# Storing the last six row tiles of a two-layer graph kernel in pairs

## The chip, the cores and the metric

The kernel runs on one core of a Trainium2 chip. The metric is the device time of that core in microseconds, from launch to end, as a median over runs. The profile adds one profiled execution, in which every instruction and every DMA packet has a time; times in the text that look like 2147.05 count from the first instruction of that execution.

## The reference

Two layers work on 3327 nodes with 512 features and a 3327x3327 adjacency matrix `adj`. Each one normalises its input, takes the positive part and adds its result to the input. Cut to what matters:

```python
# layer 0: attention with the adjacency as a bias
h = jnp.maximum(_layernorm(x, axis=-1), 0.0)
q, k, v = h @ Wq.T + bq, h @ Wk.T + bk, h @ Wv.T + bv
a = q @ k.T * scale + adj + adj
x = x + softmax(a) @ v
# layer 1: normalised graph convolution
h = jnp.maximum(_layernorm(x, axis=-1), 0.0)
A2 = adj + eye(N); d = diagonal(A2) ** -0.5
temp = A2 @ h @ W.T
x = x + relu((d[:, None] * A2 * d[None, :]) @ temp)
```

All is float32. The change concerns only the last line, and of it only the last piece that is written to the output.

## The kernel before

The 3327 rows are padded to 26 row tiles of 128 rows, and the columns of every feature matrix are handled in 128-wide pieces. The adjacency is cut into two strips of 14 and 12 tiles, and each of the three large products with it is done by a seven-product scheme (the names p1 to p7): TensorE multiplies blocks, VectorE forms sums of blocks before and after. All of these are steps of one list, `steps`; the function `run(k)` emits step k together with loads, sums and stores that were attached to it.

The order on every engine is the order in which the Python code emits instructions: the whole list is emitted under `in_order`, which ties each instruction of VectorE, TensorE, GpSimd, ScalarE and SyncE to the one emitted before it on the same engine. So each engine, and each queue of DMA issues, works through a fixed sequence. DMAs are issued by SyncE (the page calls its queue q1) and ScalarE (q10).

Stores are emitted late. A store is put on the list `posted` with a step number, and `deliver(n)` emits those whose number is below n (line 799).

Most of the output is produced transposed and is turned back in blocks of 32 by VectorE: `Columns.turn`, `Columns.scale` and `Columns.add` (lines 1151, 1157 and 1160). `Columns.add` posts four stores to SyncE (line 1163), each of 32 partitions by 28 (or 24) runs of 32 numbers, that is 128 bytes a run. The last six row tiles, 20 to 25, columns 0 to 255, take another way, since nothing is left to hide theirs: when the last product is complete, VectorE adds its last banks (line 976), TensorE turns the six tiles into six PSUM banks (`turned`, line 1111), and `finish` does the rest for one tile: ScalarE takes the positive part with the row's scale (line 1124), VectorE adds the residual `xr` (line 1125), and a store is posted (line 1126). The loop that calls it deals the six stores out in turn:

```python
for n, i in enumerate(range(20, NT)):
    finish(i, nc.scalar if n % 2 else nc.sync)
deliver(len(steps) + 1)
```

So tiles 20, 22 and 24 are stored by SyncE and tiles 21, 23 and 25 by ScalarE. Each store moves 128 runs of 1 KB, one from each partition. The residuals were loaded in pairs well before (`last_load`), so nothing here waits for them.

The completion of DMAs issued by SyncE and ScalarE is counted on eight semaphores. The programming layer hands these out in turn, over both queues, in the order in which it schedules the issues; an issue whose semaphore was last given to an earlier transfer first waits until that transfer is complete. In the built program of before, the three ScalarE stores get three of the semaphores first. Four stores of the last `Columns.add` and one earlier one then take the next five, and the three SyncE stores come round to the same three as ScalarE's: the store of tile 20 waits for the completion of that of tile 21, tile 22 for tile 23, tile 24 for tile 25.

After the last store stands a conditional branch to a general version of the kernel for unusual inputs, which is not taken for these inputs: the engines jump over it. In the block that they jump to, SyncE waits for the eight semaphores one by one (line 1720), and then all engines meet twice (line 1715).

Of the kernel before, what the change touches and what calls it, by code (L numbers as in the profile page):

```python
# [11 lines left out]
AF = mybir.ActivationFunctionType  # L12
# [3 lines left out]
P = 128  # L16
# [31 lines left out]
def graph_layers_kernel(  # L48
# [30 lines left out]
    nc = tc.nc  # L79
    NP, D = x.shape  # L80
    DC = D // P
    NT = NP // P
    scale = 1.0 / math.sqrt(D)
    E = D // 2
# [16 lines left out]
    def ring(*slots):  # L101

        turn = itertools.cycle(slots)

        def take(shape, name):
            kind, k = next(turn)
            return kind(k, shape, name)

        return take

    @contextmanager
    def in_order(*engines):

        traced = nc.cur_bb.bb.instructions
        before = traced[-1]
        yield
        begin = next(k for k in reversed(range(len(traced))) if traced[k] is before) + 1
        last = {}
        for ins in traced[begin:]:
            if ins.engine in engines:  # L120
                if ins.engine in last:
                    tc.add_manual_dep(ins, last[ins.engine].name,
                                      mybir.DependencyInfo(mybir.DependencyClass.NoSync, mybir.DependencyReason.DATA),
                                      reason="in_order")
                last[ins.engine] = ins
# [96 lines left out]
    class Chain:  # L222
# [32 lines left out]
        @staticmethod  # L255
        def finish():
            if Chain.before:
                Chain.before()
            Chain.before = None
# [377 lines left out]
    with in_order(*(e.engine for e in (nc.vector, nc.tensor, nc.gpsimd, nc.sync))):  # L637
# [9 lines left out]
        k = len(steps)  # L647
# [64 lines left out]
    sd = const.tile([P, NT], F32, name="sd")  # L712
# [79 lines left out]
    now = [0]  # L792
    posted = []
# [4 lines left out]
    def deliver(before):  # L798
        while posted and posted[0][0] < before:
            posted.pop(0)[1]()  # L800
# [19 lines left out]
    out_last = ring((half, 12), (half, 13), *spare[2:], (half, 14))  # L820
# [277 lines left out]
    xrs = {}  # L1098
# [15 lines left out]
    turned_last = {}  # L1114
# [5 lines left out]

    def finish(i, queue):

        xr, pt, o = xrs[i], turned_last[i], out_last([P, D], "r")
        nc.scalar.activation(o[:, 0:E], pt[:, 0:E], AF.Relu, scale=sd[:, i : i + 1])
        nc.vector.tensor_add(o[:, 0:E], o[:, 0:E], xr)
        posted.append((now[0], lambda: queue.dma_start(out[i * P : (i + 1) * P, 0:E], o[:, 0:E])))

    class Columns:

# [41 lines left out]
    def number_of(g, r, s, t):  # L1171
        return ((g * len(ORDER) + r) * 2 + s) * len(every) + t
# [5 lines left out]
    for g in range(3):  # L1178
        for n, r in enumerate(ORDER):
            for t, e in enumerate(every):  # L1180
                k = number_of(g, n, 0, t)
# [9 lines left out]
    for n, job in enumerate(jobs):  # L1191
        k = k0 + n * (k1 - k0) // len(jobs)
# [10 lines left out]
    k = number_of(0, 5, 1, 2)  # L1203
# [6 lines left out]
    k = number_of(1, 5, 1, 2)  # L1210
# [8 lines left out]
    k = number_of(2, 4, 0, 0)  # L1219
# [12 lines left out]
    k = number_of(1, 4, 0, 0)  # L1232
# [105 lines left out]
    with in_order(*(e.engine for e in (nc.vector, nc.tensor, nc.gpsimd, nc.scalar, nc.sync))):  # L1338
        for k in range(len(steps)):
            run(k)  # L1340
        deliver(len(steps))
        now[0] = len(steps)
        for n, i in enumerate(range(20, NT)):
            finish(i, nc.scalar if n % 2 else nc.sync)
        deliver(len(steps) + 1)
    return flags[0]

# [376 lines left out]
```

## Time and profile before

| | us |
|---|---|
| median of three runs | 2160.23 (2158.45 to 2162.33) |
| the profiled execution's own time | 2159.13 |
| its span, first to last instruction | 2157.3 |
| TensorE busy | 2137.5 (99% of the span) |
| VectorE busy | 1652.0 (77%) |
| ScalarE busy | 273.1 (13%) |
| last TensorE instruction | starts at 2146.68 |
| last VectorE addition of line 1125 | starts at 2147.95 |

The profiled execution lies 1.8 us above its span, and 1.1 us below the median of the runs. TensorE is busy nearly throughout, and only in the last ten microseconds or so is it not. In the lists of instructions a "q" after an engine's name (SPq, ACTq) marks its sequencer, which issues DMAs and waits for semaphores; for a DMA the duration is that of the issue, and the landing is given apart.

### The profile page before, as it was taken

What the parts mean: (1) busy time and instruction counts of PE and PEld (TensorE: products, weight loads), DVE (VectorE), ACT (ScalarE), POOL (GpSimd) and SP (SyncE); (2) the same over time, 40 slices, a digit from 0 to 9 for tenths busy, and PEclk for the clock granted to TensorE, in tenths of its full rate; (3) what the DMA queues carried; (4) which work ended last, traced back from release to release, by engine and by line L of the source; (5) the groups of instructions that cost most, each with busy time, mean ns of one, the idle gap of its engine ahead of it and who ended that gap; (6) DMA issues with size and microseconds to landing.
All of it is one profiled execution on the core that took longest, in us unless ns stands there. A gap on an engine that the chain in (4) does not pass through costs nothing.

```text
span 2157.3 us, 20906 instructions
## 1 busy us (share of the span) xinstructions
PE 2137.5 (99%) x6272; PEld 1180.9 (55%) x6272; DVE 1652.0 (77%) x3235; ACT 273.1 (13%) x441; POOL 68.1 (3%) x63
## 2 busy tenths in 40 slices
PE   9999999999999999999999999999999999999998
PEld 5555555555555555555454555555666665555554
DVE  7479888888887688776777778886566576778897
ACT  6311211112110000001111000010111100000000
POOL 2000000000004000000111000000000000000000
PEclk9999999999999999999999999999999999999999
DMA  8678888888999899889787889986646578978996
GB/s 305 210 257 303 296 311 282 306 289 291 337 308 299 292 370 330 278 296 309 267 308 260 303 283 368 321 303 221 203 146 201 150 225 252 303 229 247 261 293 167
DMA packets 402546, 592.10 MB, mean 274 GB/s; under 512 B 140012, under 2 KB 273528, under 8 KB 402424
## 3 DMA queue, kind: packets, MB, share of 16 engines
q1 hardware_dynamic: 374488, 533.12, 75.2%
q10 hardware_dynamic: 27936, 57.56, 7.3%
q8 instruction: 52, 0.85, 0.2%
q14 instruction: 70, 0.57, 0.1%
HBM read 422.71 MB, written 173.87 MB: 277 GB/s over the span
## 4 chain that ended last, share of the span: by engine, by line
PE 93%; DVE 4%; DMA 2%; issue 1%; POOL 0%; ACT 0%; SPq 0%; DVEq 0%
PE p L919 55%; PE Y L542 13%; PE Z L542 6%; PE p L910 5%; PE p L1026 4%; PE pw L1087 3%; PE X L542 3%; PE Y L398 2%; PE Z L398 1%; DMA rows<-row 1%; DMA part<-sum 1%; PE X L398 0%; DMA wk<-in_wk_dram 0%; DVE part L164 0%; DVE st L185 0%
## 5 line engine op out<-in xcount | busy, mean ns | idle before, releaser
L919 PE MATMUL p<-part,b 128*128 128x448 f32 (+1 forms) x3528 | 1257.6, 513 | 0.8 <-DVE part L165 0.6
L919 PEld LDWEIGHTS p<-part,b 128*128 128x128 f32 x3528 | 669.9, 190 | 542.1 <-issue 291.8
L542 PE MATMUL Y<-qt,hp 128*128 128x448 f32 (+1 forms) x832 | 308.2, 513 | 2.6 <-DVE g L546 1.8
L164 DVE TENSOR_TENSOR part<-part 128x896 f32<-128x896 f32 (+1 forms) x252 | 256.5, 1018 | 68.8 <-DMA part<-sum 29.6
L542 PEld LDWEIGHTS Y<-qt,hp 128*128 128x128 f32 x832 | 157.8, 190 | 136.3 <-issue 72.7
L542 PE MATMUL Z<-qt,hp 128*128 128x384 f32 (+1 forms) x416 | 162.3, 512 | 0.0
L166 DVE TENSOR_TENSOR part<-part,part 128x448 f32<-128x448 f32 (+1 forms) x219 | 129.4, 591 | 15.3 <-DVE part L165 0.5
L165 DVE TENSOR_TENSOR part<-part,part 128x448 f32<-128x448 f32 (+1 forms) x219 | 129.4, 591 | 7.2
L910 PE MATMUL p<-part,b 128*128 128x448 f32 (+1 forms) x336 | 124.2, 512 | 0.0
L542 PEld LDWEIGHTS Z<-qt,hp 128*128 128x128 f32 x416 | 79.0, 190 | 66.2 <-issue 37.9
L546 DVE SCALAR_TENSOR_TENSOR g<-g,Y 128x384 f32<-128x384 f32 (+1 forms) x156 | 91.3, 585 | 29.9 <-PE Y L542 28.4
L962 ACT COPY part<-p 128x384 f32<-128x384 f32 (+1 forms) x33 | 16.6, 503 | 656.1 <-PE p L919 497.8
L910 PEld LDWEIGHTS p<-part,b 128*128 128x128 f32 x336 | 63.8, 190 | 54.1 <-issue 31.0
L549 ACT ACTIVATE g<-g 128x768 f32<-128x768 f32 (+1 forms) x48 | 43.0, 896 | 347.5 <-DVE g L546 311.7
L542 PE MATMUL X<-qt,hp 128*128 128x384 f32 (+1 forms) x208 | 81.1, 512 | 0.0
L963 DVE TENSOR_TENSOR part<-p,part 128x384 f32<-128x384 f32 (+1 forms) x33 | 19.3, 585 | 62.2 <-PE p L919 61.4
L1026 PE MATMUL p<-w,ct 128*128 128x512 f32 x136 | 61.6, 592 | 0.0
L542 PEld LDWEIGHTS X<-qt,hp 128*128 128x128 f32 x208 | 39.5, 190 | 33.1 <-issue 19.3
L191 POOL TENSOR_TENSOR rstd<-ve,mhalf 128x1 f32<-128x1 f32 x46 | 38.4, 836 | 529.5 <-DVE ve L189 502.2
L982 DVE TENSOR_TENSOR ct<-p,part 128x448 f32<-128x448 f32 (+1 forms) x72 | 42.3, 608 | 16.2 <-PE p L910 12.1
L1087 PE MATMUL pw<-w,rows 128*128 128x256 f32 x208 | 53.5, 380 | 0.4 <-DVE rows L1077 0.4
L1017 DVE TENSOR_TENSOR job<-job 128x896 f32<-128x896 f32 (+1 forms) x52 | 52.9, 1017 | 0.0
(194 smaller groups left out, 1679.0 us busy)
## 6 DMA issues: line engine op xcount, KB each, us to landing
part<-sum SPq DMA_DIRECT2D x104, 448.0 KB, 5.3
part<-p SPq DMA_DIRECT2D x91, 448.0 KB, 6.0
part<-sum SPq DMA_DIRECT2D x104, 384.0 KB, 4.1
part<-p SPq DMA_DIRECT2D x91, 384.0 KB, 4.6
part<-in_adjT_dram SPq DMA_DIRECT2D x78, 448.0 KB, 5.1
b<-row SPq DMA_DIRECT2D x234, 128.0 KB, 4.9
part<-in_adjT_dram SPq DMA_DIRECT2D x78, 384.0 KB, 3.9
g<-in_adjT_dram SPq DMA_DIRECT2D x52, 448.0 KB, 4.2
```

The lines of the kernel that those rows point to most:

```text
L164: yield nc.vector.tensor_add(o[:, 0:2], g[:, 0:4:3], g[:, 1:2].to_broadcast([P, 2, g.shape[-1]]))
L165: yield nc.vector.tensor_add(o[:, 2], o[:, 1], g[:, 0])
L166: yield nc.vector.tensor_add(o[:, 3], o[:, 2], g[:, 2])
L398: nc.tensor.matmul(ps[:, :w], M[B[name]][:, c, o * P : (o + 1) * P], hp[k][:, A[name], c], start=start and c == 0, stop=c == 1, skip_group ...
L542: nc.tensor.matmul(ps[:, :wd], h_of(self.t, name, k), qt[B[name]][:, k], start=start and k == 0, stop=k == 1, skip_group_check=True)
L546: nc.vector.scalar_tensor_tensor(a[n], a[n], 2.0, ps[:, :wd], op0=ALU.mult, op1=ALU.add if sign > 0 else ALU.subtract)
L549: nc.scalar.activation(g[1], g[1], AF.Exp, **({"bias": pad} if self.t == HALF - 1 else {}))
L910: yield nc.tensor.matmul(ps[("p2", "p3", "p4", "p8")[k]][:, :w], b[:, z], a[:, 0, y], start=k == 3 and not self.seeded, stop=True, skip_gr ...
L919: yield nc.tensor.matmul(ps[r][:, :w], b[:, i], m, start=self.t == 0 and not adds, stop=self.t == PAIRS - 1 and r in ("p1", "p5", "p6", "p ...
L1017: nc.vector.tensor_add(self.a, self.a, self.b)
L1026: nc.tensor.matmul(ps, cts[s][y][d][:, k * P : (k + 1) * P], w[d], start=d == 0, stop=d == DC - 1)
L1087: nc.tensor.matmul(ps, a, W[B[name]][:, c], start=new and c == 0, stop=c == 1, skip_group_check=True)
```

## The change

The six tiles are taken two at a time. `finish` now takes the first tile of a pair, computes both into one buffer of 128 x 2 x 256, and posts one store of both. The loop runs over tiles 20, 22 and 24: the pairs 20-21 and 22-23 are stored by SyncE, the pair 24-25 by ScalarE. The ScalarE and VectorE instructions keep their number, shapes and order.

```diff
     def finish(i, queue):
 
-        xr, pt, o = xrs[i], turned_last[i], out_last([P, D], "r")
-        nc.scalar.activation(o[:, 0:E], pt[:, 0:E], AF.Relu, scale=sd[:, i : i + 1])
-        nc.vector.tensor_add(o[:, 0:E], o[:, 0:E], xr)
-        posted.append((now[0], lambda: queue.dma_start(out[i * P : (i + 1) * P, 0:E], o[:, 0:E])))
+        o = out_last([P, 2, E], "r")
+        for k in range(2):
+            nc.scalar.activation(o[:, k], turned_last[i + k][:, 0:E], AF.Relu, scale=sd[:, i + k : i + k + 1])
+            nc.vector.tensor_add(o[:, k], o[:, k], xrs[i + k])
+        to = out[i * P : (i + 2) * P, 0:E].rearrange("(k p) e -> p k e", p=P)
+        posted.append((now[0], lambda: queue.dma_start(to, o)))
...
-        for n, i in enumerate(range(20, NT)):
-            finish(i, nc.scalar if n % 2 else nc.sync)
+        for i in range(20, NT, 2):
+            finish(i, nc.scalar if i == NT - 2 else nc.sync)
         deliver(len(steps) + 1)
```

In the built program this also changes which completion semaphore each of the last transfers has. Only three stores take one now. The pair 20-21 waits for a store of the last `Columns.add` but one that was issued at 2136.56 in the profiled execution, the pair 22-23 for the one issued at 2137.15, and the pair 24-25 for one older still. The first SyncE store of a pair waits for the second addition of line 1125, the other for the fourth, and ScalarE's for the sixth.

## The prediction

> **What bounds the kernel now.** I read the page's busy line first: TensorE is busy 99% of the span, and the chain of work puts 93% of it on TensorE. The change touches no TensorE instruction, so only the stretch after the last one can move, and I went to the timeline of that stretch, then to the waits of SyncE's queue, then to the three lines that end the kernel.
>
> From the page:
>
> ```profile
> span 2157.3 us, 20906 instructions
> PE 2137.5 (99%) x6272; PEld 1180.9 (55%) x6272; DVE 1652.0 (77%) x3235; ACT 273.1 (13%) x441; POOL 68.1 (3%) x63
> ```
>
> The timeline from 2136 to 2158 us (start, duration, engine, line, what):
>
> ```profile
> 2144.19 1.94 DVE L976 TENSOR_TENSOR part<-part,p 128x384 f32<-128x384 f32 x4
> ...
> 2146.13 2.25 DVE L1125 TENSOR_TENSOR r<-r,xr 128x256 f32<-128x256 f32 x6
> ...
> 2147.05 0.35 ACTq L1126 DMA_DIRECT2D out_dram<-r  x1
> 2147.06 0.86 ACT L1124 ACTIVATE r<-pt,sd 128x256 f32<-128x256 f32 x2
> 2147.68 1.44 ACTq L1126 DMA_DIRECT2D out_dram<-r  x2
> 2150.57 2.21 SPq L1126 DMA_DIRECT2D out_dram<-r  x3
> ```
>
> VectorE has added everything at 2148.38 (2146.13 + 2.25). SyncE's three stores are nevertheless issued only from 2150.57 on, though the first needs only the first addition, done at 2146.6. The waits of SyncE's queue from 2140 to 2158 us (in total, times, longest) say why:
>
> ```profile
> SPq L1126 <- DMA out_dram<-r: 3.8, 1, 3.8
> SPq L1720 <- SPq L1720: 2.6, 1, 2.6
> ```
>
> The first SyncE store waits 3.8 us for a DMA that stores an `r`. Line 1126, by itself:
>
> ```profile
> L1126 ACTq DMA_DIRECT2D out_dram<-r x3: 348/532/707, 2147.0 to 2148.4; - x3
> L1126 SPq DMA_DIRECT2D out_dram<-r x3: 351/377/1293, 2150.6 to 2151.5; - x3
> ...
> DMA to landing us min/median/max: 2.7/3.0/3.5
> ```
>
> ScalarE's first store is issued at 2147.05 and takes the longest, 3.5 us: it lands at 2150.55, and SyncE goes on at once. That is the shared completion semaphore: tile 20's store waits for tile 21's. Last, the lines of 1720:
>
> ```profile
> L1720 SPq EVENT_SEMAPHORE  x8: 17/17/17, 2155.4 to 2156.0; - x8
> ...
> L1720 SPq COMPARE_BRANCH  x1: 50/50/50, 2152.8 to 2152.8; - x1
> ```
>
> SyncE's last issue starts at 2151.49 and lasts 1.29, to 2152.78; the branch follows; 2.6 us later come the eight waits, and 1.3 us after the last of these (2156.0) the span ends at 2157.3. So the end is SyncE's last issue plus 4.5 us. The landing of that store, 2.9 us after its issue by the DMA view (2154.4), lies hidden behind the branch.
>
> **What the Trainium skill says.** "Runtime: NRT & Kernel Launch", Instruction fetch mechanics: a taken branch whose target isn't already fetched stalls for a fetch. The trace agrees: 2.6 us between branch and first wait on SyncE, and as much on ScalarE (2149.1 to 2151.7). "DMA: Bandwidth & Descriptors", Rules for kernel authors: issuing from several engines brings no bandwidth, since all run on the same 16 DMA engines. Here, 1 KB runs went at 250 per us from ScalarE's queue nearly alone (150 packets in 2149.4 to 2150.0) and at 267 from SyncE's alone (187 in 2151.4 to 2152.1); no stretch shows both with such runs at once. "Perfetto Trace Analysis", DMA Instruction — HWDGE: the time of an issue is descriptor generation and not the movement of data. Agreed: issues take 0.35 to 1.29 us, landings 2.7 to 3.5.
>
> **The change part by part.** ScalarE's six activations and VectorE's six additions stay as they are, so 2148.38 stays: nothing gained, nothing lost. The two-tile buffer costs no new wait, since the first activation waits for TensorE alone in both programs.
>
> *SyncE's wait of 3.8 us goes.* The pairs wait for column stores issued at 2136.56 and 2137.15; line 1163's landings take 7.7 us at most, so these are complete by 2145. What is late next is the addition. The pair 20-21 needs the second one, as ScalarE's first store does now, so it can start where that one starts, at 2147.05; SyncE's column stores are issued by then (the last starts at 2145.88 and takes 0.83: 2146.71). That costs the pair a later addition than tile 20 had, hidden as long as SyncE is busy until 2146.71, so 0.3 us at most. The pair 22-23 needs the fourth: 2147.68. ScalarE's pair needs the sixth: 2148.41.
>
> *Three SyncE issues become two, of twice the runs.* Stores of two runs from each partition are in the trace: line 534 takes 359/367/633 ns (least, median, most). With 0.37 each, SyncE is done at 2147.68 + 0.37 = 2148.05. Bounds: 0.36 from below, and from above 1.29, as before's last issue, which gives 2149.0. In before it was 2152.78: 4.7 us earlier. With the tail unchanged at 4.5 us the end would be 2152.6, and SyncE would reach its eight waits at 2148.05 + 2.65 = 2150.7.
>
> *The cover of the landings is now thin.* SyncE no longer gives the data 2.6 us more than they need. The DMA view counts 475 packets of SyncE's queue in 2148 to 2149 and 56 in the next: some 530 of the column stores' 128-byte runs are left at 2148.0. In 2147 to 2148, with the queue alone, 1248 went. So they are gone at 2148.4. Then come 6 x 128 = 768 runs of 1 KB. SyncE's queue has the engines alone until ScalarE's pair begins; a 1 KB store begins about 0.9 us after its issue (2150.57, none before 2151.3), so at 2149.3: 0.9 us x 267 = 240 runs. The other 528 share the engines. Alone, a queue kept them busy 69% (250 per us) and 75% (267), so two can reach 357 per us if they fill each other's gaps: 1.5 us, to 2150.8. If they don't, 528 / 260 = 2.0 us, to 2151.3. A landing is reported some 0.5 us after its last data (ScalarE's last: data thin out after 2150.5, landing 2148.41 + 2.7 = 2151.1). So all land between 2151.3 and 2151.8. The three semaphores concerned stand fourth to sixth of the eight; from the sixth to the end are 0.15 + 1.3 = 1.5 us. End between 2152.8 and 2153.3, and 2152.6 if landings don't show at all.
>
> *Sum.* The span of 2157.3 becomes 2152.6 to 2153.3, so 4.0 to 4.7 us less. I take 4.45, near the end where the two queues overlap, because each alone leaves a quarter of the engines' time unused. The profiled execution took 2159.13, so it would be 2154.7; the median is 1.1 above it: 2160.23 - 4.45 = 2155.8.
>
> **The rivals.**
>
> *A late landing takes the place of the wait.* Some of the 16 parts of a transfer come late. For it: line 1126's landings already spread over 0.8 us, and line 534's two-run stores take 4.7 us in the median and 8.1 at most; the three engines' branches fetch in these very microseconds. Against it: line 534 ran amid heavy traffic. With 4.7 us from 2147.68 or 2148.41 the landing is 2152.4 to 2153.1 and the end 2153.9 to 2154.6: 2.7 to 3.4 us gained, so 2157.2 us. With 8.1 from 2148.41 it is 2156.5, the end 2158.0, a loss of 0.7.
>
> *SyncE's issues stall behind the column stores: slower.* Issues of line 1163 took 2.57 at 2128.05 and 2.73 at 2130.66, when much was queued. At 2147.05 some 1780 runs are still queued. Two issues of 2.7 us end at 2152.45, still 0.3 us before 2152.78. It decides from 5.7 us for both on; with 5.49 each, the longest issue of any SyncE row (line 830), they end at 2158.0 and the kernel takes 2165.5. Against it: the fourth column store of the last group, issued at 2145.88 with most of the other three still queued, took only 0.83.
>
> *The wait stays.* If something else than the shared semaphore holds SyncE, the first pair goes at 2150.57, the second at 2150.94, done at 2151.3 instead of 2152.78: 1.5 us gained, 2158.7. Against it: the landing at 2150.55 fits too well.
>
> **How the numbers follow.** A measurement of this kernel can tell about 0.2%, 4.3 us, from no change; the first case lies across that bound. Its chance is 0.75, the late landing's 0.18, the stall's 0.04 and the wait that stays 0.03. In the first case the gain is 4.45 at best knowledge, a little over 4.3, and the medians scatter (the three runs by 3.9 us): I give 0.51 to over the bound and 0.24 to within it. With the late landing 0.03 is over it by scatter, 0.15 within. The stall counts as slower. So 0.54 faster, 0.42 same, 0.04 slower. The range: 4.0 to 4.7 widened by a scatter of 2 us gives 2153.5 to 2158.2, and the late landing and the wait that stays reach to 2158.7.
>
> **What would show it.** Right: no wait of SyncE's queue for an `r` store; its two issues near 2147.05 and 2147.7, its branch near 2148.1, and a wait at line 1720 of up to 1 us for landings. Late landing: that wait is longer. Stall: issues of over 1.3 us at line 1128. The forecast is wrong if the last TensorE instruction moves by more than a microsecond, or SyncE's first pair starts after 2149.

## The result, and the profile after

The changed kernel takes 2157.2 us in the median of 22 runs, against 2160.17 for 22 runs of the kernel before: a ratio of 0.9986, 95% interval 0.9981 to 0.9992. That is 3.0 us less, 1.7 to 4.1 by the interval: a gain, and one within the 0.2% (4.3 us) named in the prediction. Forecast were 2155.8 us in a range of 2153.5 to 2158.7.

The span of its profiled execution says much less:

```profile
span 2156.7 us, 20900 instructions
PE 2139.1 (99%) x6272; PEld 1180.4 (55%) x6272; DVE 1651.7 (77%) x3235; ACT 273.1 (13%) x441; POOL 68.0 (3%) x63
```

That is only 0.6 us under before's 2157.3, because the long stretch in front, which the change does not touch, differed from one execution to the other: the sixth addition of line 1126 ends at 2150.93 here, and ended at 2148.38 in before. What lies behind that addition is what the change can reach. I call the time from its end to the end of the span **the tail**, and give times of the tail as T+. The tail was 2157.34 - 2148.38 = 9.0 us before and is 2156.72 - 2150.93 = 5.8 us now: 3.2 us less, which fits the medians.

The timeline of the end of the changed kernel (start, duration, engine, line, what):

```profile
2148.68 2.25 DVE L1126 TENSOR_TENSOR r<-r,xr 128x256 f32<-128x256 f32 x6
2149.50 1.31 SPq L1128 DMA_DIRECT2D out_dram<-r  x2
2150.96 0.40 ACTq L1128 DMA_DIRECT2D out_dram<-r  x1
```

SyncE's two stores now begin while VectorE still adds, 1.4 us before the last addition ends; in before the first of three began at T+2.2. The waits of SyncE's queue from 2148 us on:

```profile
SPq L1722 <- SPq L1722: 3.9, 1, 3.9
SPq L1128 <- DVE r L1126: 1.0, 2, 0.5
```

The 3.8 us for another store's landing are gone. A store now waits for VectorE's additions, 0.5 us each time. But the branch, 2.6 us in before, stands at 3.9. Lines 1128 and 1722:

```profile
L1128 SPq DMA_DIRECT2D out_dram<-r x2: 554/568/583, 2149.5 to 2150.2; - x2
L1128 ACTq DMA_DIRECT2D out_dram<-r x1: 401/401/401, 2151.0 to 2151.0; - x1
...
DMA to landing us min/median/max: 3.9/3.9/3.9
```

```profile
L1722 SPq EVENT_SEMAPHORE  x8: 17/17/17, 2154.8 to 2155.3; - x8
...
L1722 SPq COMPARE_BRANCH  x1: 50/50/50, 2150.9 to 2150.9; - x1
```

SyncE branches at 2150.9 (T-0.1; in before T+4.5) and is at its eight waits at 2154.8 (T+3.9). It goes through them without a stop, one each 0.07 to 0.09 us. ScalarE's pair, issued at 2150.96, lands 3.9 us later, at 2154.85 (T+3.9). So the landings stay hidden, by some 0.3 us only, and the branch still sets the end.

### The profile page after: what moved, and what is told of

It is laid out like the page before. It is cut to its first block, busy times and chain, and to the rows that moved or that the text cites. A ratio compares the mean times of both kernels' runs of the same rounds, so it can differ in the third digit from the quotient of the medians.

```text
span 2156.7 us, 20900 instructions
## 1 busy us (share of the span) xinstructions
PE 2139.1 (99%) x6272; PEld 1180.4 (55%) x6272; DVE 1651.7 (77%) x3235; ACT 273.1 (13%) x441; POOL 68.0 (3%) x63
## 4 chain that ended last, share of the span: by engine, by line
PE 90%; DMA 5%; DVE 5%; issue 1%; POOL 0%; ACT 0%; SPq 0%; ACTq 0%; DVEq 0%
PE p L919 52%; PE Y L542 13%; PE Z L542 6%; PE p L910 5%; PE p L1026 4%; PE pw L1087 3%; PE X L542 3%; PE Y L398 2%; DMA rows<-row 1%; PE Z L398 1%; DMA part<-sum 1%; DMA t<-b 1%; DMA part<-p 1%; DVE part L164 1%; PE X L398 0%
```

## The experiments

Two theories on the gain: **the wait** on the shared completion semaphore was its cause, or **the number** of transfers (three instead of six) was. And two questions behind it: why the branch now takes 3.9 us, and what comes next if it goes.

**Does it repeat?** The changed kernel and the kernel before, once more each.

> The changed kernel once more, to see how far its one profile holds. I measure the tail: from the end of the sixth addition on VectorE to the end of the span, 8.9 us in the profile of before and 5.7 in that of the changed kernel. If the tail is settled by the program, it is 5.5 to 6.0 again, with 3.9 us between SyncE's branch and its first wait, and the median about 3 us under before. If the 3.9 us were a chance of one execution (2.6 in before), the tail is near 4.5 here.

Measured: ratio 0.9979 (0.9972 to 0.9986), 2155.41 against 2159.67 us, so 4.3 us less where the first measurement had 3.0. The tail is 6.1 us, and the branch is long again:

```profile
SPq L1722 <- SPq L1722: 4.3, 1, 4.3
```

So the long branch belongs to the program and is no chance of one execution.

> The kernel before once more, for a second profile of its end. If its tail is settled by the program it is 8.5 to 9.3 us again, with SyncE's first store 2.0 to 2.4 us after the sixth addition and 2.6 us of branch. If the first profile had an unlucky late landing and a long last issue, the tail is near 7.5.

Measured: tail 9.5 (a little over the 8.5 to 9.3 expected), SyncE's first store at T+2.2, branch 2.6 us. Its last issues again took long, 1.4 and 0.7 us. Between the two kernels the tails differ by 2.9 to 3.7 us over the four profiles.

**The wait or the number?** First the six single stores without the wait:

```diff
-            finish(i, nc.scalar if n % 2 else nc.sync)
+            finish(i, nc.sync)
```

> Six stores of one tile each, as before, but all issued by SyncE, so that none waits for the completion of a store issued a moment ago. If the wait on the shared semaphore is what the pairs took away, this gains nearly as much as the pairs: SyncE's last issue starts right after the sixth addition, 0.3 to 0.6 us later than with the pairs, and the tail is 6.0 to 6.5, the median 2.4 to 3.0 under before. If the gain came from having three transfers instead of six, it is lost: tail near 8.9, median as before.

Measured: ratio 0.9990 (0.9984 to 0.9997), 2157.4 against 2159.67 us; tail 7.8. Neither expectation holds. The wait is gone, but SyncE's six issues follow one another from 2146.34 to 2150.56 (T+2.7):

```profile
2146.34 4.22 SPq L1126 DMA_DIRECT2D out_dram<-r  x6
```

They take 0.7, 0.6, 0.9, 0.7, 0.4 and 0.4 us, the first four while column stores are still queued. SyncE becomes the bound, and its branch takes 3.2 us. Then the pairs with one transfer more, so that the third SyncE store comes round to ScalarE's semaphore:

```diff
+        if i == 22:
+            for k in range(2):
+                posted.append((now[0], lambda k=k: queue.dma_start(to[:, k], o[:, k])))
+            return
         posted.append((now[0], lambda: queue.dma_start(to, o)))
```

> The pairs, but the middle pair (tiles 22 and 23) stored by SyncE as two single tiles: four transfers, three of them on SyncE. SyncE's third then comes round to the semaphore of ScalarE's pair and waits for its landing. If the wait is the cause, SyncE's last issue goes to about 3.9 us after the sixth addition, the branch follows without much traffic in 2.6 us, and the tail is 8.6 to 9.2: the whole gain is gone, the median within 1 us of before. If the number of transfers is the cause, four instead of three cost a sixth to a third of the gain: tail 6.2 to 6.8.

The waits of SyncE's queue in this kernel:

```profile
SPq L1130 <- DMA out_dram<-r: 3.5, 1, 3.5
SPq L1726 <- SPq L1726: 2.5, 1, 2.5
```

The wait is back, with 3.5 us, and the branch is down to 2.5. The last store is issued at T+3.6, the tail is 8.4, a little under the expected 8.6, and the ratio 0.9995 (0.9986 to 1.0003): no gain that can be told from none. By the tail, four transfers with the wait lose 2.3 to 2.6 us of the 2.9 to 3.7 that three without it gained. Six transfers without the wait gain only 1.1 to 1.7. So neither theory is enough alone: the gain needs both, no wait and few issues. The six singles also moved three stores from ScalarE to SyncE; six stores shared by both queues, without the wait, were not run.

**Where do SyncE's and ScalarE's shares matter?** Two splits of the three pairs:

```diff
-            finish(i, nc.scalar if i == NT - 2 else nc.sync)
+            finish(i, nc.sync if i == 20 else nc.scalar)   # a4
+            finish(i, nc.scalar)                           # c1
```

> The pairs, but SyncE issues only the first and ScalarE the other two. SyncE branches some 0.7 us earlier. If the end is set by SyncE's branch with its 3.9 us, the tail shrinks to 5.1. If the landings stand right behind it, SyncE now waits for ScalarE's last pair, which lands 3.9 us after the sixth addition as in the changed kernel, and the tail stays at 5.4 to 5.8: no gain over the pairs.

Measured: ratio 0.9984 (0.9978 to 0.9991), tail 5.5. SyncE branches at T-0.75, takes 3.9 us all the same, and then stops 0.2 us for ScalarE's last pair, which lands at T+3.8. The second expectation holds. The very last that SyncE waits for is ScalarE's branch, which follows an issue of 1.3 us:

```profile
SPq L1717 <- ACTq L1722: 0.2, 1, 0.2
```

> The pairs, all three issued by ScalarE, so that SyncE branches right after its column stores, some 1.5 us ahead of the pairs' data. If data in flight are what makes a branch slow, SyncE's takes under 3.3 us here and SyncE is at its waits before the landings; ScalarE, which branches last and amid the data, sets the end: tail 5.0 to 5.5, up to 0.8 us better than the pairs and no more than a median can show. If ScalarE's issues stall behind the column stores as SyncE's do (0.5 to 0.9 us each), its branch is later and the tail is 5.7 or more.

Measured: ratio 0.9984 (0.9978 to 0.9991), tail 5.6, between the two expected. SyncE branches at T-1.6, ahead of the pairs' data, in 2.9 us. The last pair lands at T+4.2, and SyncE's wait for it sets the end; ScalarE, after an issue of 1.2 us, is through its branch at T+4.7, just before SyncE asks for it. Neither split can be told from the pairs as they are.

**Why does the branch take 3.9 us?** Three suspects: the stores' data, the column stores still queued, and the other engines, which branch at about the same time. The first kernel stores only 64 of the 256 columns of the six tiles and leaves the others unstored:

```diff
-        posted.append((now[0], lambda: queue.dma_start(to, o)))
+        posted.append((now[0], lambda: queue.dma_start(to[:, :, 0:64], o[:, :, 0:64])))
```

> The pairs, but of each of the six last tiles only 64 of the 256 columns are stored (the others are left out): the same issues and branches, a quarter of their bytes. In the changed kernel SyncE needs 3.9 to 4.3 us from its branch to its first wait, in before 2.6. If the stores' own data in flight delay that, it falls to 2.6 to 3.0 here and the tail from 5.8 to 4.4 to 4.8. If it is the branches of the other engines at the same moment, it stays at 3.7 to 4.3 and the tail at 5.5 to 6.0. If it is the column stores that are still queued, it also stays.

Line 1722 of this kernel:

```profile
L1722 SPq EVENT_SEMAPHORE  x8: 17/17/17, 2153.7 to 2154.2; - x8
...
L1722 SPq COMPARE_BRANCH  x1: 50/50/50, 2150.8 to 2150.8; - x1
```

The same branch at the same place (T-0.0) takes 2.9 us, and the tail is 4.8. The issues, the column stores and the other engines' branches stand where they stood, so the stores' bytes are what lengthens it, by this one profile. The other two suspects were tried as well. First the other engines: VectorE and ScalarE get more work before their branches.

```diff
         deliver(len(steps) + 1)
+        spin, spin2 = half(7, [P, 1024], "spin"), half(3, [P, 1024], "spin2")
+        for k in range(4):
+            nc.vector.memset(spin, 0.0)
+        for k in range(10):
+            nc.scalar.copy(spin2[:, 0:E], turned_last[25][:, 0:E])
```

> The pairs, and after the last addition VectorE clears a spare buffer four times and ScalarE copies a bank ten times, so that these two branch some 3 us later; nothing of the stores changes. If the engines' branches at the same moment delay one another, SyncE's branch takes 2.6 to 3.2 us here. If traffic delays it, it stays at 3.7 to 4.3. The tail says nothing here, since the two late engines set it (7 us or more).

```profile
L1727 SPq EVENT_SEMAPHORE  x8: 17/17/17, 2152.1 to 2152.6; - x8
...
L1727 SPq COMPARE_BRANCH  x1: 50/50/50, 2148.2 to 2148.2; - x1
...
L1727 DVEq COMPARE_BRANCH  x1: 72/72/72, 2151.9 to 2151.9; - x1
L1727 ACTq COMPARE_BRANCH  x1: 54/54/54, 2152.5 to 2152.5; - x1
...
L1727 ACTq EVENT_SEMAPHORE  x1: 17/17/17, 2155.1 to 2155.1; - x1
```

VectorE and ScalarE branch 3.7 and 4.3 us after SyncE, and SyncE's branch still takes 3.9. ScalarE's own, when all data have moved, takes 2.6. So VectorE and ScalarE are not the reason. (TensorE branches earlier in every kernel and was not moved.) Then the column stores: the last four are left out.

```diff
             r0 = (STRIPS[self.s] + self.y * HT[self.s]) * P
+            if (self.s, self.y, self.d) == (0, 1, 1):
+                return
             for of, rows in self.parts(self.o, out[r0 : r0 + H[self.s]]):
```

> The pairs, but the last four column stores, the ones issued just ahead of the pairs, are left out. If their 3584 short runs delay the branch and the landings, SyncE's branch takes 2.6 to 3.0 us here, the last pair lands under 3 us after its issue and the tail is 4.4 to 4.8. If the branches of the engines delay one another, the branch stays at 3.7 to 4.3 and the tail at 5.5 to 6.0.

Measured: SyncE's branch 4.0 us, tail 6.2, ScalarE's pair lands 3.75 us after its issue. The first expectation falls: the short runs in front are not the reason. The tail even grew a little: SyncE's second issue took 0.9 us, so its branch began only at T+0.3. ScalarE's branch took 4.6 us. Why these two took so long is not settled.

Side by side, SyncE's branch and the bytes of all these stores that had not yet begun to move when it began, counted from the packets in the traces:

| kernel | KB left | branch, us |
|---|---|---|
| pairs, one store more | 128 | 2.5 |
| before, two profiles | 145, 140 | 2.6, 2.6 |
| pairs, a quarter of the data | 218 | 2.9 |
| six singles on SyncE | 252 | 3.2 |
| pairs without last column stores | 528 | 4.0 |
| pairs, two profiles | 796, 803 | 3.9, 4.3 |
| pairs, the others branch late | 803 | 3.9 |
| pairs, two on ScalarE | 885 | 3.9 |
| pairs, all on ScalarE | 1008 | 2.9 |

The last row stands apart: its branch begins before any pair is issued and spends its first half with column stores alone. In four rows (a quarter of the data, pairs, the others branch late, two on ScalarE) part of the pairs is issued up to 0.8 us after the branch began. The kilobytes left are no rule for every engine either: in before, ScalarE's branch begins with 632 KB left, 342 of which begin to move while it runs, and takes 2.6 us.

The traces show where the time goes. They list packets of two queues of the kind "instruction", q8 and q14, and in the three profiles of the kernels without the branch (below) none of these stands in the tail. Where the others branch late, SyncE branches at 2148.22 and is at its waits at 2152.07. The queues' packets that begin in 2148.22 to 2150.45, and then in 2150.45 to 2152.07 (packets, MB, share of the engines):

```profile
q1 hardware_dynamic: 809, 0.54, 82.0%
q10 hardware_dynamic: 110, 0.11, 14.3%
```

```profile
q10 hardware_dynamic: 162, 0.15, 27.1%
q1 hardware_dynamic: 26, 0.02, 4.2%
q8 instruction: 1, 0.02, 3.9%
q14 instruction: 1, 0.01, 1.2%
```

In before SyncE branches at 2152.83; the same for 2152.83 to 2153.7, and for 2153.7 to its first wait at 2155.41:

```profile
q1 hardware_dynamic: 145, 0.14, 50.6%
```

```profile
q1 hardware_dynamic: 19, 0.01, 2.0%
q14 instruction: 1, 0.01, 1.6%
```

Four profiles have just one q14 packet between SyncE's branch and its first wait, and two of them, both of before, no q8 packet there. So I take the q14 packet for the fetch of SyncE's target:

| kernel | from branch to packet, us | from packet to first wait, us | branch, us |
|---|---|---|---|
| before, two profiles | 0.93, 0.94 | 1.66, 1.66 | 2.6, 2.6 |
| pairs, all on ScalarE | 1.34 | 1.57 | 2.9 |
| pairs, the others branch late | 2.28 | 1.57 | 3.9 |

All that the branch grows by lies before this packet begins. It also explains the row that stood apart: there the packet begins before the first 1 KB run does. Which store packets hold it up, and on which DMA engines, the trace does not tell; that it queues behind them is my reading.

**What if the branch is not there?** The general version is left out of the program, for the pairs and for the six single stores:

```diff
-            with tc.If(graph_layers_kernel(tc, x_in, xT_in, *rest, out, bad, n) > 0):
-                general_kernel(tc, x_in[:n], adj_in, *rest, out[:n])
+            graph_layers_kernel(tc, x_in, xT_in, *rest, out, bad, n)
```

> The pairs without the branch: the general version of the kernel is left out of the program. If the landings stand right behind the branch, SyncE waits for ScalarE's pair (3.9 us after the sixth addition) and the tail is 5.1 to 5.6: the branch's 3.9 us bring 0.3 us at most. If the branch is what is to be shortened, the tail falls to 4.6 or less.

> The kernel before (six single stores) without the branch: the general version of the kernel is left out. Its wait on the shared semaphore stays, so SyncE's last issue ends about 4.4 us after the sixth addition and its data land at 6.0. Without a branch the end follows the last landing by 1.0 us, as it did with the pairs: tail about 7.0. The pairs without branch had 4.4, so the gain of the pairs without a branch is 2.6 us. If the wait only mattered because it delayed the branch, the two are within 0.5 us.

> The six single stores without the branch once more. In its first profile the tail was 5.0 us and SyncE's first store came 1.4 us after the sixth addition, against 2.2 in before, so the branches' fetches seemed to delay the stores too. If so, 4.8 to 5.4 and 1.2 to 1.6 again. If that was chance, SyncE's first store is at 2.0 to 2.4 and the tail near 6.

The pairs: ratio 0.9973 (0.9962 to 0.9984), tail 4.4. The singles: ratio 0.9980 (0.9974 to 0.9987), tail 5.0, and 5.1 once more. For the pairs the second expectation holds (4.6 or less). The singles are 2 us shorter than the 7.0 expected, and within 0.7 us of the pairs. SyncE's waits and line 1126 of the singles without branch, first profile:

```profile
SPq L1126 <- DMA out_dram<-r: 3.0, 1, 3.0
```

```profile
L1126 SPq DMA_DIRECT2D out_dram<-r x3: 351/377/404, 2149.2 to 2150.1; - x3
...
DMA to landing us min/median/max: 1.7/2.0/2.7
```

The wait is there, but ends at T+1.4 instead of T+2.2, none of the three issues is long, and the stores land in 1.7 to 2.7 us, where before had 2.7 to 3.5 (2.1 to 3.5 in its second profile). The landing of ScalarE's pair shortens too, from 3.9 to 3.4 us. So stores and branches slow each other, in both directions. And of the pairs' gain without a branch only 0.6 to 0.7 us is left (5.0 and 5.1 against 4.4): I read this so that the DMA engines have ScalarE's data and the column stores to move while SyncE waits, and that the wait was dear in before because the branch stood behind it. No run shows this by itself.

## Why the prediction was right or wrong, point by point

**Right: the stretch, and the wait.** Only the tail moved. SyncE's wait of 3.8 us for the store of tile 21 is gone, and what is late next is the addition, as worked out: the two stores begin 1.4 and 0.7 us before the last addition ends (forecast 1.3 and 0.7). SyncE's last issue ends at T-0.1, where T-0.3 was forecast, since issues take 0.55 to 0.58 and not 0.37. That is 4.5 us earlier than in before; the step said 4.7.

**Wrong in size: the tail behind the last issue.** The step "with the tail unchanged ... SyncE would reach its eight waits at 2148.05 + 2.65" carried the branch over from before. There it ran with 145 KB left to move. Here nearly all stores were still to move, and it took 3.9 us. That is 1.3 us: of the 4.5 us that SyncE was earlier, 3.2 are left in the tail. A sign of it was in the profile of before, in the same list of line 1720 from which the prediction took SyncE's and ScalarE's 2.6 us:

```profile
L1720 DVEq COMPARE_BRANCH  x1: 72/72/72, 2148.0 to 2148.0; - x1
...
L1720 DVEq EVENT_SEMAPHORE  x1: 21/21/21, 2151.4 to 2151.4; - x1
```

VectorE's branch, amid the stores, took 3.4 us there. With the pairs it took 3.7 us, and 3.0 when all data had moved.

**Wrong in size: the landings.** They were set at T+2.9 to T+3.4 (2151.3 to 2151.8) and came at T+3.9. In the sum this is hidden, but barely: with a branch of 2.6 us the landing alone would have given 3.9 + 1.5 = 5.4 us of tail, so 3.6 us gained. Both terms had to be right for 4.45. The overlap of the two queues itself came out. In the 1.2 us from T+1.2 on (2152.13 to 2153.33), with both at work:

```profile
DMA packets 419, 0.43 MB, mean 359 GB/s; under 512 B 19, under 2 KB 416, under 8 KB 416
q1 hardware_dynamic: 248, 0.24, 59.4%
q10 hardware_dynamic: 168, 0.17, 40.4%
```

Without the 19 short packets and three larger ones these are 397 runs of 1 KB, 331 per us against 357 forecast; without the branch they were 364 per us. What was late were its beginning and its end. The column runs, which the forecast had gone at T+0, came thinly until T+1.1 (191 of them began after T+0), and the last 98 runs of 1 KB, begun after T+2.4, ended only at T+3.5. Without the branch the data end at T+3.1 and ScalarE's pair lands at T+3.4, the late edge of the forecast.

**The rivals.** "A late landing takes the place of the wait" named 2157.2 us, which is what was measured, with 4.7 us for a landing where 3.9 was found. Its wait did not appear, since the branch was longer still. Its number came out by another route, the branch, so that the number fits is luck. The stall behind the column stores did not occur with the pairs. It did, in a mild form, with six singles on SyncE, whose issues took up to 0.9 us. The wait that stays was excluded at once by SyncE's waits. The likelier side, a gain of over 0.2% (chance 0.54), did not come: the gain is within it by the median and at its edge by the second measurement (ratio 0.9979). That the second median, 2155.41 us, lies so close to the forecast 2155.8 does not make the 4.45 us right, since the tails differ by 2.9 to 3.7 us in every pair of profiles.

**What would show it.** Of the signs named, the two issues and the branch right after the last addition came out. The wait at line 1722 for landings did not.

## What to carry to other kernels

When an issue waits for a transfer that has nothing to do with it, look for a completion semaphore that comes round; one transfer less or more can take the wait away or bring it back, and one more brought it back here. Before a stretch is moved earlier, ask what its cover did while it ran: a fixed-looking cost behind it, such as a taken branch, was measured in quiet and may now fall amid the data. Other engines may already pay it amid data in the same profile, so look at theirs too. Compare short ends by aligning the profiles at the last common instruction, since here the stretch in front differed by more than the effect.

## What the runs showed of the hardware

A taken branch took SyncE 2.5 to 2.6 us with at most 145 KB of stores left to move and 3.9 to 4.3 us with 528 to 885 KB left; with 1008 KB, none of the pairs issued yet, it took 2.9 us. The Trainium skill ("Runtime: NRT & Kernel Launch", Instruction fetch mechanics) says that the target is fetched by DMA. The traces agree: in the four profiles where it can be told apart, a packet of an instruction queue began 0.9 us after the branch with little left to move and 2.3 us after it amid the pairs' data, and SyncE went on 1.6 to 1.7 us after the packet began.

In return the stores of 128 KB landed in 2.1 to 3.5 us beside branches and in 1.7 to 2.8 us without. An issue of 128 runs by SyncE, 0.35 to 0.40 us at the least, took 0.6 to 0.9 us in the six singles while short runs were queued. But SyncE's last issues in before took 0.7 to 1.4 us with no column store left to move, so these runs are not the only cause.
